# A relational graph layer on one core: one edge tile in 26 fetched row by row instead of one in 28, stores held back, first indices by their own transfer

## The chip, the core and the metric

The kernel runs on one core of a Trainium2 chip. The core has five engines that run side by side and meet at semaphores: TensorE (PE in the profile; PEld is its weight load), VectorE (DVE), ScalarE (ACT), GpSimd (POOL) and SyncE (SP). DMA transfers are issued from the queues of SP, ACT and POOL. The metric is the device time of one execution in microseconds (us); less is better. A time is given as the median of several runs.

## What is computed

The layer takes 12,500 nodes with 256 features, 212,500 edges sorted by destination, and one of 8 relations for each edge. `h` is the normalized and rectified input. An edge brings the row of its source, multiplied by the weight of its relation, to its destination; the node's own row goes through a ninth weight.

```
h = jnp.maximum(_layernorm(x, axis=-1), 0.0)
hx = jnp.einsum('ni,rio->rno', h, weight)
msg = hx[edge_type, src]
agg = jax.ops.segment_sum(msg, dst, num_segments=num_nodes)
out = x + agg * 0.5 ** 0.5 + h_bias + (h @ loop_weight) * 0.5 ** 0.5
```

## The kernel before

**Edges.** The order of sum and product is turned round: source rows are summed for each (destination, relation) first, and the sums are multiplied by the weights once for each group of nodes. The edges stand in 789 units of two tiles with 128 edges each, 1578 tiles in all (the first 80 units are cut plainly, the others overlap a little, so that each covers a narrow range of destinations). For each tile the 128 source rows of 1 KB are brought into one slot of `msg`. There are 66 slots, in pairs of tiles that rotate. VectorE makes one-hot matrices for four tiles at once (`onehots`, L998). TensorE multiplies a tile's rows by its one-hot matrix, four times 128x128 (`edge_sums`, L1036), which sorts them into columns by destination and relation, and VectorE adds a unit's result to the ring of sums `acc` (`add_sums`, L1069).

**Two ways of fetching rows.** Nearly all tiles come by `gather` (L941): one indirect DMA of POOL, which reads 128 row numbers from a column of `gidx` and writes the tile's slot. Every 28th tile (`SINGLE = 28`, tile 27, 55, ...) is left out by POOL. `begin_fetch` books it `FAR = 36` tiles ahead: SP and ACT take 64 of its rows each, load the row numbers into registers, 32 at a time (`load_sources`, L962), and issue a DMA for each row (L970), four items for each queue and tile of the loop (`FETCH`), from `HOLD = 8` tiles after the booking. This begins at tile 152, when the normalized table `h32` is complete for it, and stops 16 tiles before the end. The first 88 tiles are gathered from `x` and normalized in place by ACT (L874); the others are gathered from `h32`.

**How far POOL may run ahead.** `goal(t)` lets the gathers be 64 tiles ahead of the loop at first, fewer later, at least 24, and near the end 8. Each gather also waits for the sums of the unit that stands last in the program before it ("no faster than the sums").

**Groups.** When a group of 128 nodes has its last edge (98 groups, some 16 tiles apart), its products are queued between the edge tiles: two with the loop weight `wl`, then sixteen with `w` (`product`, L1243), into one of two PSUM tiles `po`. Three tiles after the last product `finish` adds bias and result to the rows of x (L1231, L1258) and stores them: four groups at once (L1263), or one by one for the last six and the short first one (L1260). These stores are issued on SP, where the row fetches stand too, and where a store waits until VectorE has added the result. For the last group the products with `wl` stand behind all products of the group before it. At the beginning everything waits for the indices: three transfers on SP (L391), then a cast (L468), a transpose on TensorE and a cast (L432) that make `gidx`, and then POOL's first gather.

**The order of the work** is written by hand in one loop over tiles: a tile's fetches, its sums, then what `issue` takes from the queue of products by a budget, then the late steps such as `finish`.

Of the kernel before, what the change touches and what calls it, by code (L numbers as in the profile page):

```python
# [12 lines left out]
I32 = mybir.dt.int32  # L13
# [7 lines left out]
SP = mybir.EngineType.SP  # L21
# [39 lines left out]
NEXT = 24  # L61
CLOSE = 8

SINGLE = 28
FETCH = 4
SOURCES = 32
BY_SP = (0, 2)
HOLD = 8
FAR = 36
COUNTERS = 4  # L70
LANDINGS = 68

# [177 lines left out]
def kernel(  # L250
# [78 lines left out]
    with ExitStack() as main:  # L329
# [28 lines left out]
        outs = [ps_o.tile([P, 2, D], F32, name=f"po{i}") for i in range(2)]  # L358
        msg, oh, offsets, kind = {}, {}, {}, {}
        firsts, stops, loops, marked, typed, gidx, col = {}, {}, {}, {}, {}, {}, {}  # L360
        added, zeroed, listed = {}, {}, set()
        single, fetches = {}, {SP: [], ACT: []}
        counters = [tc.alloc_semaphore(f"rows{i}") for i in range(COUNTERS)]
        fetched, summed = {}, {}
        landings = [tc.alloc_semaphore(f"landed{i}") for i in range(LANDINGS)]
# [561 lines left out]
        def gather(t):  # L927
            if t % PAIR == 0 and t not in msg:
                room(t)
            if t % QUAD:  # L930
                kind[t] = kind[t - 1]
            else:
                kind[t] = "h" if state["h32"] is not None and t >= state["h32"] + LATE else "x"
            table = {"h": h32, "x": x}[kind[t]]
            b, i, u = place_of(t)
            if single_rows(t) and t not in fetched and t - done["tile"] >= FAR:
                begin_fetch(t)
            if t in fetched:
                return
            at = i * P + u  # L940
            i = nc.gpsimd.indirect_dma_start(  # L941
                out=msg[t], out_offset=None, in_=table[:, :],
                in_offset=bass.IndirectOffsetOnAxis(ap=gidx[b][:, at : at + 1], axis=0))
            if kind[t] == "h":
                n = landed[t] = len(landed)
                i.then_inc(landings[n % LANDINGS], 16)
                tc.no_tile_sem_insts.add(i.ins.name)
                tc.add_to_no_dep_group(f"landed{t}", i.ins)
            if "unit" in latest:
                tc.add_manual_dep(  # L950
                    i.ins, latest["unit"], SYNC_DEP, reason="no faster than the sums")
# [261 lines left out]
        def wrap(g):  # L1213
# [3 lines left out]
            tc.add_manual_dep(i.ins, added[plan.last[g]].name, SYNC_DEP, reason="sums complete")  # L1217
            nc.vector.memset(acc[:, :, :, RING : RING + WIN], 0.0)

        def group_work(g):  # L1220

            d0 = plan.starts[g]
# [10 lines left out]
            def product(r, c, g=g):  # L1233
                n = plan.ends[g] - plan.starts[g]
                if (r, c) == (R, 0):
                    got["out", g] = outs[g % 2][:, 0, :]
                if r == R:
                    while ("self", g) not in got:
# [12 lines left out]
                    tc.add_manual_dep(i.ins, added[plan.last[g]].name, SYNC_DEP, reason="sums complete")  # L1251

            def finish():
                q, k = divmod(g, XG)
                rows_ = got["x", q]
                if g != final:
                    biased(g)
                nc.vector.tensor_add(rows_[:n, k, :], rows_[:n, k, :], got["out", g][:n])  # L1258
                if XG * (q + 2) >= plan.NG or n < P:
                    nc.sync.dma_start(out[d0 : d0 + n], rows_[:n, k, :])  # L1260
                elif k == XG - 1:
                    first = plan.starts[XG * q + shorts(q)]
                    nc.sync.dma_start(  # L1263
                        out[first : d0 + n].rearrange("(k p) d -> p k d", p=P), rows_[:, shorts(q) :, :])
                b = g + SLOTS
                q, k = divmod(b, XG)
                if b < plan.NG:
                    if q < plan.typed:
                        clear(b)
                    else:  # L1270
                        begin(b)
                if q + 1 >= plan.typed and XG * (q + 1) < plan.NG:
                    if k == max(XG // 4, SLOTS - XG * q):
                        load_groups("h", h32, q + 1)
                    if k == XG - 2:
                        mark(q + 1)
                    if k == XG - 1:
                        find_types(q + 1)
# [7 lines left out]
                    work.append((0.55, lambda r=r, c=c: product(r, c)))  # L1286
            work.append((0.0, last))
            if final is not None and g == final - 1:
                work.append((0.0, lambda: biased(final)))
                for c in range(KC):  # L1290
                    work.append((0.55, lambda c=c: product(R, c, final)))
            return work

        with tc.manual_schedule():

            load = prepare(0)
            load[0]()
            for i in range(STAGED):
                load_rows(i)
# [10 lines left out]
            nc.vector.memset(ones_b, 1.0)  # L1310
            nc.vector.memset(zero, 0.0)
            head = len(sources(0, {}))
            for f in load[1 : 1 + head]:
                f()
            for t in range(min(STARTED, NT)):
                gather(t)
            gathered = min(STARTED, NT)

# [127 lines left out]
            for t in range(NT):  # L1446
# [3 lines left out]
                while gathered < min(NT, goal(t)):  # L1450
                    gather(gathered)
                    gathered += 1
                fetch(FETCH)
                blocks_ahead(t)
                credit = min(0.0, credit) + SHARE - (0.52 if t % PAIR else 0.0)
# [78 lines left out]
                step()  # L1534
            while held():
                advance(None)
            state["general"] = nc.values_load(flag[0:1, 0:1], min_val=0, max_val=1)
            while queue or late:
                if late:
                    late.pop(0)[1]()  # L1540
                else:
                    queue.pop(0)[3]()


    with tc.If(state["general"]):
# [26 lines left out]
```

## Time and profile before

| | us |
|---|---|
| median of 3 runs | 1940.45 |
| lowest and highest | 1939.35, 1941.13 |
| the profiled execution, own time | 1939.95 |
| its span, first to last instruction | 1938.2 |

The span is 1.75 us less than the profiled execution's own time, which holds what lies around the program too. In the rows of the profile a line number such as L941 is a line of the kernel; `msg<-h,gidx` names what is written and read; in brackets stands the idle time of the engine before the instruction, and what ended it. "issue" stands for time in which the engine waited for nothing that the profile shows. The mean granted clock of TensorE was 0.955 of full speed. The lines that matter are shown with the prediction.

### The profile page before, as it was taken

The numbers are of one execution on the slowest core, as the hardware profiler recorded it, in microseconds if no ns is written. First come the engines' busy times: TensorE is split into PE (matmuls) and PEld (weight loads), VectorE is DVE, ScalarE is ACT, GpSimd is POOL, SyncE is SP. The second block draws the span as 40 slices with busy tenths as digits, with TensorE's granted clock in tenths as the row PEclk, the third lists the DMA queues.
The fourth block names the chain that finished last, engine by engine and source line by source line (L and its number), as shares of the span: only waits on it lengthen the run. The fifth ranks groups of instructions, "written<-read, shape, count | busy, mean of one in ns | idle before, by whom it ended". The sixth has DMA issues, their size and how long they took to land.

```text
span 1938.2 us, 40494 instructions
## 1 busy us (share of the span) xinstructions
PE 1693.9 (87%) x10152; PEld 1455.2 (75%) x10152; DVE 1315.0 (68%) x3304; ACT 136.4 (7%) x290; POOL 1453.3 (75%) x1554
## 2 busy tenths in 40 slices
PE   2368999999898899889899989898898989899998
PEld 1357889899887787777777778677777778777887
DVE  7879668976667865657766557775566786565543
ACT  6974000000000000000000000000000000000000
POOL 7777777777777777777777777777777777777775
PEclk9568999999999999999999999999999999999999
DMA  9964444444454444453444444444444444444432
GB/s 319 385 216 138 138 132 131 142 134 143 121 154 131 121 142 131 122 150 111 141 132 121 141 132 130 134 118 142 131 120 136 128 135 132 123 141 127 132 118 87
DMA packets 158466, 279.13 MB, mean 144 GB/s; under 512 B 35487, under 2 KB 109330, under 8 KB 158226
## 3 DMA queue, kind: packets, MB, share of 16 engines
q0 software_dynamic: 73344, 200.38, 35.5%
q1 hardware_dynamic: 76744, 72.84, 12.0%
q10 hardware_dynamic: 8138, 3.30, 0.9%
q8 instruction: 80, 1.31, 0.3%
q14 instruction: 160, 1.31, 0.2%
HBM read 250.78 MB, written 25.60 MB: 143 GB/s over the span
## 4 chain that ended last, share of the span: by engine, by line
PE 37%; DMA 22%; POOL 19%; DVE 9%; issue 9%; ACT 3%; SPq 1%; DVEq 0%; POOLq 0%; ACTq 0%; PEldq 0%
DMA msg<-h,gidx 20%; POOL msg L941 19%; PE po L1243 19%; PE ps L1036 17%; DVE acc L1069 2%; ACT msg L874 1%; DVE oh L998 1%; DVE stats L830 1%; SPq L970 1%; DVE acc L1111 1%; ACT xt L874 1%; DVE moves L456 1%; DMA w<-in_L_gnn_weight_dram 1%; DMA xt<-in_x_dram 1%; PE pt L1093 1%
## 5 line engine op out<-in xcount | busy, mean ns | idle before, releaser
L941 POOL DMA_INDIRECT msg<-h,gidx x1440 | 1367.7, 950 | 439.9 <-issue 374.9
L1036 PEld LDWEIGHTS ps<-oh,msg 128*128 128x128 f32 x6312 | 924.9, 197 | 380.0 <-DMA msg<-h,gidx 247.0
L1036 PE MATMUL ps<-oh,msg 128*128 128x136 f32 (+1 forms) x6312 | 1001.9, 289 | 198.8 <-DMA msg<-h,gidx 122.9
L1243 PE MATMUL po<-w,acc 128*128 128x256 f32 (+1 forms) x3136 | 888.7, 389 | 8.7 <-DVE acc L1069 8.3
L1069 DVE TENSOR_TENSOR acc<-acc,ps 128x352 f32 x789 | 408.2, 517 | 387.5 <-PE ps L1036 376.6
L1243 PEld LDWEIGHTS po<-w,acc 128*128 128x128 f32 (+1 forms) x3136 | 519.1, 193 | 47.5 <-issue 11.9
L1111 DVE SCALAR_TENSOR_TENSOR acc<-types,pt 128x256 f32<-128x256 bf16 x720 | 259.6, 414 | 65.5 <-PE pt L1093 55.5
L998 DVE TENSOR_TENSOR oh<-fixed,cols 128x544 f32<-128x544 f32 x395 | 282.7, 716 | 0.0
L1243 PE MATMUL po<-wl,self_t 128*128 128x256 f32 (+1 forms) x392 | 113.5, 415 | 7.9 <-DVE self_t L1098 3.0
L941 POOL DMA_INDIRECT msg<-in_x_dram,gidx x88 | 83.7, 951 | 28.6 <-issue 23.4
L1243 PEld LDWEIGHTS po<-wl,self_t 128*128 128x128 f32 (+1 forms) x392 | 72.4, 206 | 17.2 <-DVE self_t L1098 4.4
L1231 DVE TENSOR_TENSOR xr<-xr,po 128x256 f32<-128x256 f32 (+1 forms) x98 | 40.6, 414 | 16.1 <-PE po L1243 16.1
L1165 DVE CAST types<-pt 128x512 bf16<-128x512 f32 x23 | 15.9, 690 | 50.8 <-PE pt L1161 50.8
L1258 DVE TENSOR_TENSOR xr<-xr,po 128x256 f32<-128x256 f32 (+1 forms) x98 | 41.2, 421 | 10.6 <-PE po L1243 7.3
L874 ACT ACTIVATE msg<-msg,shift,rstd 128x256 f32<-128x256 f32 x88 | 44.8, 587 | 5.0 <-DVE stats L838 3.4
L456 DVE TENSOR_SCALAR moves<-fixed 128x271 int32<-128x271 int32 (+1 forms) x90 | 40.7, 452 | 3.8 <-DVE acc L1069 2.4
L1093 PE MATMUL pt<-ident,hr 128*128 128x128 f32 (+1 forms) x196 | 38.5, 279 | 5.4 <-DVE self_t L1098 2.4
L1098 DVE COPY self_t<-pt 128x256 f32<-128x256 f32 (+1 forms) x98 | 40.8, 416 | 2.8 <-PE ps L1036 1.8
L458 DVE COPY_PREDICATED fixed<-moves,fixed 128x311 int32<-128x311 int32 (+14 forms) x90 | 38.0, 422 | 3.1
L874 ACT ACTIVATE xt<-xt,shift,rstd 128x256 f32<-128x256 f32 x66 | 33.7, 587 | 10.4 <-DVE shift L871 10.4
L1093 PEld LDWEIGHTS pt<-ident,hr 128*128 128x128 f32 (+1 forms) x196 | 25.6, 150 | 7.6 <-DVE self_t L1098 2.5
L1149 DVE TENSOR_TENSOR of<-pt,line 22x512 bf16<-22x512 f32 x23 | 15.7, 682 | 20.7 <-PE pt L1142 20.6
(168 smaller groups left out, 368.1 us busy)
## 6 DMA issues: line engine op xcount, KB each, us to landing
msg<-h ACTq DMA_DIRECT2D x3200, 1.0 KB
msg<-h SPq DMA_DIRECT2D x3200, 1.0 KB
msg<-h,gidx POOLq DMA_INDIRECT x1440
hr<-h SPq DMA_DIRECT2D x23, 512.0 KB
xr<-in_x_dram SPq DMA_DIRECT2D x23, 512.0 KB
out_dram<-xr SPq DMA_DIRECT2D x22, 512.0 KB
xt<-in_x_dram SPq DMA_DIRECT2D x16, 512.0 KB
h<-xt SPq DMA_DIRECT2D x16, 512.0 KB
```

The source lines that it names most:

```text
L456: nc.vector.tensor_single_scalar(m, packed[:, :n], 1 << (bit + k), op=ALU.bitwise_and)
L874: nc.scalar.activation(row, row, AF.Relu, bias=shift[:n, j : j + 1], scale=rstd[:n, j : j + 1])
L941: i = nc.gpsimd.indirect_dma_start(out=msg[t], out_offset=None, in_=table[:, :], in_offset=bass.IndirectOffsetOnAxis(ap=gidx[b][:, at : at ...
L998: j = nc.vector.tensor_tensor(o[:, k : k + v, :i, :width], iota_f[:, :width].unsqueeze(1).unsqueeze(1).to_broadcast([P, v, i, width]), of. ...
L1036: j = nc.tensor.matmul(ps[:, c, first : first + width], m[:, c * P : (c + 1) * P], o[:, :width], start=(i == 0 and c == 0), stop=(end and ...
L1069: i = nc.vector.tensor_tensor(a, a, ps, op=ALU.add)
L1093: in_run("turns", nc.tensor.transpose(pst[:, c, :n], rows_[:n, c * P : (c + 1) * P], ident[:n, :n]), c == KC - 1)
L1098: nc.vector.tensor_copy(got["self", g][:, :, :n], pst[:, :, :n])
L1111: i = nc.vector.scalar_tensor_tensor(acc[:, :, r, s0 : s0 + n], of, float(r + 1), pst[:, :, :n], op0=ALU.is_equal, op1=ALU.mult)
L1231: nc.vector.tensor_add(rows_[:n, k, :], rows_[:n, k, :], outs[g % 2][:n, 1, :])
L1243: i = nc.tensor.matmul(got["out", g][:n], lhs, rhs, start=(r == R and c == 0), stop=(r == R - 1 and c == KC - 1))
L1258: nc.vector.tensor_add(rows_[:n, k, :], rows_[:n, k, :], got["out", g][:n])
```

## The change

One tile in 26 is fetched row by row (`SINGLE`), and booked 40 tiles ahead (`FAR`). The stores of four groups are put on SP's queue 44 tiles of the loop after their sums (`STORE`). The first unit's row numbers come by a transfer of their own on ACT's queue into `direct`, and the first two gathers read them there and are issued before the other indices are turned. The last group's two products with `wl` go to the front of the work of the group before it (with a loop that first issues the `finish` of the group that used the same PSUM tile), and the two stores of the groups before the last are held until all edges are summed.

```
-SINGLE = 28
+SINGLE = 26
-FAR = 36
+FAR = 40
+STORE = 44
...
+            of = direct[:, i : i + 1] if t < PAIR else gidx[b][:, at : at + 1]
             i = nc.gpsimd.indirect_dma_start(
                 out=msg[t], out_offset=None, in_=table[:, :],
-                in_offset=bass.IndirectOffsetOnAxis(ap=gidx[b][:, at : at + 1], axis=0))
+                in_offset=bass.IndirectOffsetOnAxis(ap=of, axis=0))
...
+        def behind(i):
+
+            tc.add_manual_dep(i.ins, latest["unit"], SYNC_DEP, reason="behind the last edges")
...
                 if (r, c) == (R, 0):
+                    while g == final and final - 2 not in finished:
+                        late.pop(0)[1]()
                     got["out", g] = outs[g % 2][:, 0, :]
...
             def finish():
+                finished.add(g)
...
-                if XG * (q + 2) >= plan.NG or n < P:
+                if final is not None and g in (final - 2, final - 1):
+                    alone = rows_[:n, k, :]
+                    stores.append((NT, lambda: behind(nc.sync.dma_start(out[d0 : d0 + n], alone))))
+                elif XG * (q + 2) >= plan.NG or n < P:
                     nc.sync.dma_start(out[d0 : d0 + n], rows_[:n, k, :])
                 elif k == XG - 1:
                     first = plan.starts[XG * q + shorts(q)]
-                    nc.sync.dma_start(
-                        out[first : d0 + n].rearrange("(k p) d -> p k d", p=P), rows_[:, shorts(q) :, :])
+                    to, of = out[first : d0 + n].rearrange("(k p) d -> p k d", p=P), rows_[:, shorts(q) :, :]
+                    stores.append((done["tile"] + STORE, lambda: nc.sync.dma_start(to, of)))
...
             if final is not None and g == final - 1:
+                work = [(0.55, lambda c=c: product(R, c, final)) for c in range(KC)] + work
                 work.append((0.0, lambda: biased(final)))
-                for c in range(KC):
-                    work.append((0.55, lambda c=c: product(R, c, final)))
...
             load = prepare(0)
+            direct = const.tile([P, PAIR], I32, name="direct")
+            with nc.allow_non_contiguous_dma(reason="one unit's indices, a column a tile"):
+                nc.scalar.dma_start(direct, src[:U].rearrange("(i p) -> p i", p=P))
             load[0]()
...
+            for t in range(PAIR):
+                gather(t)
             for f in load[1 : 1 + head]:
                 f()
-            for t in range(min(STARTED, NT)):
+            for t in range(PAIR, min(STARTED, NT)):
                 gather(t)
...
+                while stores and stores[0][0] <= t:
+                    stores.pop(0)[1]()
                 fetch(FETCH)
```

How this moves instructions is seen in the program's order, engine by engine. POOL from its last set-up to the end of the gathers, before and after (`direct` is the new tile of row numbers, `h_57` the table `h32`):

```order
L1304 IOTA tid 128x1
L1305 IOTA tid 128x6
L1307 MEMSET wraps 128x1 x17
L941 DMA msg<-in_x_dram,gidx 128x256 x88
L941 DMA msg<-h_57,gidx 128x256 x1440
```

```order
L1318 IOTA tid 128x1
L1319 IOTA tid 128x6
L1321 MEMSET wraps 128x1 x17
L943 DMA msg<-in_x_dram,direct 128x256 x2
L943 DMA msg<-in_x_dram,gidx 128x256 x86
L943 DMA msg<-h_57,gidx 128x256 x1435
```

Two gathers no longer depend on `gidx`, and there are 1435 gathers from the table instead of 1440.

TensorE in the last 14 tiles, where the products of the last group but one (`po_134`) stand between the edge tiles (`ps`); `po_135` is the last group. Before:

```order
L1036 MATMUL ps_121<-oh,msg 128x104 x2
L1243 MATMUL po_134<-wl,self_t 128x256 x2
L1243 MATMUL po_134<-w,acc 128x256 x2
L1036 MATMUL ps_122<-oh,msg 128x136 x2
L1243 MATMUL po_134<-w,acc 128x256 x4
L1036 MATMUL ps_122<-oh,msg 128x104 x2
L1243 MATMUL po_134<-w,acc 128x256 x4
L1036 MATMUL ps_119<-oh,msg 128x136 x2
L1243 MATMUL po_134<-w,acc 128x256 x3
L1036 MATMUL ps_119<-oh,msg 128x104 x2
L1243 MATMUL po_134<-w,acc 128x256 x3
L1036 MATMUL ps_120<-oh,msg 128x136 x2
```

After:

```order
L1038 MATMUL ps_121<-oh,msg 128x104 x2
L1251 MATMUL po_135<-wl,self_t 128x256 x2
L1251 MATMUL po_134<-wl,self_t 128x256 x2
L1038 MATMUL ps_122<-oh,msg 128x136 x2
L1251 MATMUL po_134<-w,acc 128x256 x4
L1038 MATMUL ps_122<-oh,msg 128x104 x2
L1251 MATMUL po_134<-w,acc 128x256 x4
L1038 MATMUL ps_119<-oh,msg 128x136 x2
L1251 MATMUL po_134<-w,acc 128x256 x3
L1038 MATMUL ps_119<-oh,msg 128x104 x2
L1251 MATMUL po_134<-w,acc 128x256 x3
L1038 MATMUL ps_120<-oh,msg 128x136 x2
```

The last group's loop products now stand ahead of the other's, and the first product with `w` stands one edge tile later. Before, the loop products of the last group stood behind the last row shown.

SP at the end of the changed program, where the rows of the last fetched tile (1559) stand between stores (L1272 stores a group by itself, L1276 four groups, L1270 a held one):

```order
L1188 DMA xr<-in_x_dram 128x2x256
L964 TENSOR_LOAD single
L972 DMA msg<-h_57 1x1024 x11
L1272 DMA out_dram<-xr 128x256
L972 DMA msg<-h_57 1x1024 x21
L964 TENSOR_LOAD single
L972 DMA msg<-h_57 1x1024 x30
L1276 DMA out_dram<-xr 128x4x256
L972 DMA msg<-h_57 1x1024 x2
L1272 DMA out_dram<-xr 128x256
L1270 DMA out_dram<-xr 128x256 x2
```

Of that tile's 64 rows on SP, 53 stand behind the store of group 93, and the two held stores stand behind all rows. Before, the last fetched tile was 1539, and four stores of single groups in a row ended the queue.

More of the change, by code (lines that the diff above doesn't have):

```diff
@@ L360 @@
         firsts, stops, loops, marked, typed, gidx, col = {}, {}, {}, {}, {}, {}, {}
-        added, zeroed, listed = {}, {}, set()
-        single, fetches = {}, {SP: [], ACT: []}
+        added, zeroed, listed, finished = {}, {}, set(), set()
+        single, fetches, stores = {}, {SP: [], ACT: []}, []
         counters = [tc.alloc_semaphore(f"rows{i}") for i in range(COUNTERS)]
@@ L1542 @@
                     queue.pop(0)[3]()
+                while stores:
+                    stores.pop(0)[1]()
     with tc.If(state["general"]):
```

2 lines of the change are left out of this document (added).

## The prediction

> **What bounds the kernel now.** I read the page's shares first, then who waits for whom, then one line's own times, then the stretches.
>
> ```profile
> PE 1693.9 (87%) x10152; PEld 1455.2 (75%) x10152; DVE 1315.0 (68%) x3304; ACT 136.4 (7%) x290; POOL 1453.3 (75%) x1554
> ...
> L941 POOL DMA_INDIRECT msg<-h,gidx x1440 | 1367.7, 950 | 439.9 <-issue 374.9
> ```
>
> By busy share TensorE (PE) looks like the bound, 87% against 75% for GpSimd (POOL). But the 439.9 us of idle before POOL's gathers end in "issue", which is no wait. The list of POOL's waits says it more sharply (engine and line, released by: us in total, times, longest):
>
> ```profile
> POOL msg L941 <- issue: 398.4, 1306, 0.3
> POOL msg L941 <- PE ps L1036: 48.5, 159, 0.3
> ...
> POOL msg L941 <- ACT msg L874: 2.4, 6, 0.9
> ```
>
> The longest gap is 0.3 us whoever is named, with one exception of 0.9. So POOL hands out one gather after the other, 0.95 us each and 0.30 us between. The view of line 941 gives the pace:
>
> ```profile
> L941 POOL DMA_INDIRECT msg<-h,gidx x1440: 942/946/1279, 115.2 to 1921.5; - x180
> ```
>
> From the first start of these 1,440 gathers to the last: (1921.5 - 115.2) / 1439 = **1.2553 us a gather**, the few that take up to 1279 ns included. With 88 gathers from x ahead of them this train runs from 4.7 us to 1922.5 us and has no hole worth a name. The stretches (us; busy time and count of PE, PEld, DVE, ACT, POOL; granted clock, DMA share, GB/s) show where PE stands:
>
> ```profile
> 4.72:166.00 161.28, 73.92 (x335) 64.21 (x336) 133.84 (x473) 122.40 (x260) 121.73 (x128) 0.70 0.89 296
> 166.00:550.00 384.00, 368.99 (x2385) 337.97 (x2383) 287.71 (x703) 12.67 (x30) 290.69 (x306) 0.98 0.47 134
> 550.00:1900.00 1350.00, 1218.52 (x7255) 1024.53 (x7254) 881.69 (x2099) 0.00 (x0) 1021.93 (x1076) 0.98 0.45 131
> ```
>
> Until 166 us PE is held up by the normalizing and the weights and falls behind the gathers; to 550 us it works without a break (369 of 384 us) to catch up; from there it has 10% to spare (1218.5 of 1350 us) and follows the gathers. So a gather less is worth its 1.2553 us, as long as PE's spare time lasts, and what speeds PE up alone is worth nothing before the last few us.
>
> **The change, part by part.**
>
> *One tile in 26.* Tiles 25 + 26k replace 27 + 28k. The first allowed tile is 152 (4-tile rows from 92 - 4 + 64), the last is 1561, so k runs from 5 to 59: 55 tiles instead of 50. The order has 2 + 86 + 1435 = 1523 gathers against 1528. Five fewer: 5 x 1.2553 = **6.28 us off POOL's train**. Their 640 rows go to SP and ACT. What those pay:
>
> ```profile
> L970 SPq DMA_DIRECT2D msg<-h x3200: 227/228/1044, 209.7 to 1871.4; - x189
> ```
>
> A fetched tile costs each queue 64 issues of this line, and two loads of row numbers ahead of them. A slow stretch of SP, quoted with the rivals below, took 13.85 us for 35 rows with such a load among them, 0.396 us a row; at that pace 64 rows take 25.3 us, and 26 tiles last 25 x 1.2553 = 31.4 us. The rows fit, so I take nothing for them. Without that cover PE would wait for the tile's last rows, but POOL is allowed 24 tiles of lead there and would not feel it before PE is some 20 us late.
>
> *Stores 44 tiles later, fetches begun 40 tiles ahead instead of 36.* SP's own waits, longest in total first:
>
> ```profile
> SPq L1263 <- DVE acc L1069: 185.1, 14, 20.0
> SPq L1263 <- DVE xr L1258: 171.4, 9, 57.1
> SPq L1260 <- DVE xr L1258: 88.1, 5, 30.3
> ```
>
> Before, SP stands at a store until its four groups are summed (185.1 + 171.4 us in 23 waits), with the row fetches queued behind it. After, the sums are 44 tiles old when SP comes by, the store waits for nothing, and rows land earlier. That moves waits of SP, and PE's on fetched tiles; neither is on POOL's path: 0. What could be late next is a load into a buffer that a held store still reads; in the new order such a load stands about 27 tiles (some 33 us) of row issues behind that store, so 0 as well.
>
> *First unit's indices by a transfer of their own.* The start, in order of time (start, duration):
>
> ```profile
> 2.87 0.29 DVE L468 CAST sf<-nat_s 128x256 f32<-128x256 int32 x1 [1.72 <-DMA nat_s<-in_src_dram]
> ...
> 4.01 0.42 DVE L432 CAST gidx<-pt 128x256 int32<-128x256 f32 x1 [0.84 <-PE pt L428]
> ...
> 4.72 1.11 POOL L941 DMA_INDIRECT msg<-in_x_dram,gidx  x1 [2.10 <-DVE bound_o L1325]
> ```
>
> POOL waits 2.10 us for the turned indices, so it is free at 4.72 - 2.10 = 2.62. The kernel's first transfer lands at 2.87; one issued at the same moment on ACT's queue, 256 pieces of 4 bytes, the trace does not show. Bounds: it lands with that one and saves up to those 2.10 us, or it is later than 4.72 and costs. I take a start near 3 us. Two gathers then last to 5.5, past 4.43, where the turned indices are ready for the third. But does a start 1.8 us earlier reach the end? Here is the exception of 0.9 us:
>
> ```profile
> 158.36 1.22 PE L1243 MATMUL po<-w,acc 128*128 128x256 f32 x2 [6.51 <-DVE acc L1069]
> ...
> 164.18 0.95 POOL L941 DMA_INDIRECT msg<-h,gidx  x1 [0.30 <-issue]
> 165.54 0.63 PE L1036 MATMUL ps<-oh,msg 128*128 128x136 f32 x4
> 166.02 0.94 POOL L941 DMA_INDIRECT msg<-h,gidx  x1 [0.89 <-ACT msg L874]
> ```
>
> Counted from the start, the gather at 166.02 is that of tile 128. By the order it may not pass tile 63's sums (64 tiles of lead), and PE runs those until 166.0, having stood 6.51 us behind VectorE's bookkeeping just before. POOL lost 0.89 - 0.30 = 0.59 us there already. PE's date at tile 63 comes from weights, norms and VectorE; the gathers are 60 tiles ahead of it. So an earlier start is waited away at this place: **0**, with 2.10 us for the range. Without this wait the gain would be the full 1.8.
>
> *Last loop product sooner, two stores held.* The tail:
>
> ```profile
> 1895.55 0.73 PE L1036 MATMUL ps<-oh,msg 128*128 128x136 f32 x4 [0.66 <-DMA msg<-h,gidx]
> ...
> 1906.49 0.95 POOL L941 DMA_INDIRECT msg<-h,gidx  x1 [0.30 <-issue]
> ...
> 1909.44 0.69 PE L1036 MATMUL ps<-oh,msg 128*128 128x104 f32 x4 [0.71 <-DMA msg<-h,gidx]
> ...
> 1911.30 1.13 PE L1243 MATMUL po<-w,acc 128*128 128x256 f32 x4 [0.29 <-DVE acc L1215]
> ...
> 1921.46 4.19 PE L1036 MATMUL ps<-oh,msg 128*128 128x104 f32 x28
> 1921.51 0.95 POOL L941 DMA_INDIRECT msg<-h,gidx  x1 [0.30 <-issue]
> ...
> 1926.27 7.17 PE L1243 MATMUL po<-w,acc 128*128 128x256 f32 x32 [0.61 <-DVE acc L1069]
> ```
>
> PE last waits for a gather at 1909.44 (tile 1565, twelve before the last), and from there works through but for 0.29 and 0.61 us. The moved product, as many matmuls of the same size as those at 1911.30, now stands ahead of them and fills the 0.29. Nothing else changes in length: **0.29 us**. The price beside it: the last fetched tile, 1559, now lies between PE's wait at 1895.55 and the one at 1909.44. Gather 1565 comes 1.26 us sooner against PE's work there, but PE idled only 0.71 us for it: 1.26 - 0.71 = **0.55 us given back**. The last gather is no new bound: 1921.51 + (1909.44 - 1906.49) = 1924.46, and PE reaches that tile 24/28 through the 4.19 us, at 1925.05. The two held stores are issued after the last edges and before the last sum is ready, while PE is in its 7.17 us: 0.
>
> *Sum.* 6.28 + 0 + 0.29 - 0.55 = 6.02 us. The profiled execution took 1939.95 us (span 1938.2), so 1933.93; the median of the runs is 0.5 us above it, and **1934.4 us** is my forecast, 0.31% faster. What a measurement can tell here is about 0.2%, that is 3.9 us.
>
> **The rivals.**
>
> *The early start passes through.* If tile 63 is done sooner than in the profiled execution, the 1.8 us survive: 1932.6. For it: the wait cost only 0.59 us, and a date that norms and weights set need not be the same in every execution (the three runs span 1.8 us). Against: nothing in the change helps the norms.
>
> *PE takes over.* If PE's spare time is gone where the later fetched tiles fall, for instance because TensorE's clock drops there (0.70 up to 166 us, 0.98 later), POOL's gain of three of five tiles is given back: 2 x 1.2553 = 2.5 us left, 1937.9. Against it stand the 10% of idle from 550 us on.
>
> *The transfers, not their issue, set the pace.* Then rows moved to other queues bring nothing: 1940.4. For it speaks 0.89 of DMA share up to 166 us; against, 0.45 later, where all fetched tiles are, and POOL's even step of 0.95 + 0.30 us. The Trainium skill's page DMA: Bandwidth & Descriptors, section "Issuing engines are not separate DMA queues", states that issuing on several engines saves only the sequencer's time, which is usually small beside the transfer; read alone, it speaks for this case, and by it the sum would be 0. The rows say that here this small time, 1.25 us a tile, is what everything waits for.
>
> *Slower: the last fetched tile comes late.* In the new order 53 rows of tile 1559 stand on SP behind the store of group 93, which waits for that group's sum:
>
> ```profile
> 1854.10 13.85 SPq L970 DMA_DIRECT2D msg<-h  x35
> ...
> 1867.87 0.42 DVE L1258 TENSOR_TENSOR xr<-xr,po 128x256 f32<-128x256 f32 x1
> ```
>
> With this sum ready at 1868.3 the rows are out 53 x 0.396 = 21.0 us later, and landed, with 2.95 us, at 1892.3. PE comes to that tile near 1901 (evenly between 1895.55 and 1909.44): cover 9 us. Beyond that each us is a us at the end; against the time before it decides from 15 us late. The longest wait of such a store was 30.3 us; 10 us more than cover and gain, 25 us late, gives 1950. Against: that sum would have to be later than anything in the tail shows.
>
> **How the numbers follow.** My forecast 0.66, the early start 0.13, PE taking over 0.11, transfers 0.04, the late tile 0.06. The lower end is 1940.45 - 6.28 - 0.29 - 2.10 = 1931.8; the upper one is the second rival, 1937.9; that leaves out the last two cases and little more. Faster by over 0.2% means below 1936.6: the forecast nearly whole, the early start, a little of the second rival, 0.77. Within 0.2%: most of that rival, the transfers, 0.16. Slower: 0.07.
>
> **What would show it.** In the changed kernel's profile: 1,435 + 88 gathers at 1.25 us; the first gather at about 3 us, and at tile 128 a wait grown to 2 us or more, the gather still at 166; SP's waits at stores nearly gone; PE's last wait for a gather before tile 1565 or none there, the wait for line 1215's counterpart gone. I am wrong if POOL shows gaps for PE after 166 us, if the gathers' mean step grows, or if PE waits for fetched rows in the last 100 us.

## The result and the profile after

| | before | changed |
|---|---|---|
| median of 15 runs each, us | 1939.98 | 1935.58 |
| lowest and highest | 1939.05, 1941.55 | 1934.37, 1937.89 |
| the profiled execution (its span) | 1939.95 (1938.2) | 1936.13 (1934.4) |

The ratio is 0.9977, 95% interval 0.9969 to 0.9985: the change makes the kernel 4.4 us, or 0.23%, faster. The forecast was 1934.4 us.

The page's shares, the view of the gathers' line and the list of POOL's waits in the changed kernel (us in total, times, longest):

```profile
PE 1685.5 (87%) x10152; PEld 1479.8 (77%) x10152; DVE 1316.3 (68%) x3304; ACT 136.3 (7%) x290; POOL 1449.5 (75%) x1549
```

```profile
L943 POOL DMA_INDIRECT msg<-h,gidx x1435: 942/946/1273, 115.1 to 1916.2; - x180
```

```profile
POOL msg L943 <- issue: 398.5, 1306, 0.3
...
POOL msg L943 <- PE ps L1038: 48.9, 158, 1.0
...
POOL msg L943 <- ACT rstd L867: 1.5, 2, 1.2
```

POOL still hands out one gather after the other. The train's last gather starts at 1916.2 instead of 1921.5. That is 5.3 us, about the five gathers; the profiled time fell by only 3.8 us. So some 1.5 us were lost behind the last gather, 1.1 of them until the end of PE's last product. The train itself has two longer gaps than before, of 1.0 and 1.2 us. Both stand at the beginning, as the timeline shows (start, duration, engine and line, in brackets the idle time before it and what ended it):

```profile
3.67 1.11 POOL L943 DMA_INDIRECT msg<-in_x_dram,direct  x1 [1.05 <-DMA direct<-in_src_dram]
5.08 0.94 POOL L943 DMA_INDIRECT msg<-in_x_dram,direct  x1 [0.30 <-issue]
...
34.61 0.94 POOL L943 DMA_INDIRECT msg<-in_x_dram,gidx  x1 [1.02 <-PE ps L1038]
...
164.25 0.94 POOL L943 DMA_INDIRECT msg<-h,gidx  x1 [1.16 <-ACT rstd L867]
165.50 0.94 POOL L943 DMA_INDIRECT msg<-h,gidx  x1 [0.30 <-issue]
166.75 0.94 POOL L943 DMA_INDIRECT msg<-h,gidx  x1 [0.31 <-ACT msg L875]
```

The first gather starts 1.05 us earlier (3.67 against 4.72). 0.72 us of it (1.02 - 0.30) are waited away at 34.61, where the gather of tile 24 may not pass the first unit's sums, and 0.86 us at 164.25, at tile 126. Counted from the start, the gather of tile 128 stands at 166.75; before it stood at 166.02.

SP no longer stands at the four-group stores (before: 185.1 and 171.4 us at L1263). Its longest waits are now for PE's sums ahead of a row and for single stores near the end:

```profile
SPq L972 <- PE ps L1038: 85.0, 18, 41.9
SPq L1272 <- DVE xr L1267: 75.6, 3, 39.5
```

PE in the tail of the changed kernel:

```profile
1885.24 0.69 PE L1038 MATMUL ps<-oh,msg 128*128 128x104 f32 x4 [0.45 <-DMA msg<-h,gidx]
...
1890.43 3.02 PE L1038 MATMUL ps<-oh,msg 128*128 128x136 f32 x12 [1.88 <-DMA msg<-h,gidx]
1893.24 1.35 PE L1251 MATMUL po<-wl,self_t 128*128 128x256 f32 x4
...
1906.31 1.91 PE L1251 MATMUL po<-wl,self_t 128*128 128x256 f32 x8
...
1922.05 7.17 PE L1251 MATMUL po<-w,acc 128*128 128x256 f32 x32 [0.61 <-DVE acc L1071]
```

PE last waits for a gather at 1890.43, and for 1.88 us, longer than any wait in the tail before. From there it works without a gap but for the 0.61 us at 1922.05. The wait for L1215's counterpart is gone: the two loop products of the last group now run with the others at 1906.31. Three tiles (x12) at 1890.43 take 3.02 us, though, and the loop products at 1893.24 take 1.35 us where four of the same took 1.03 before:

```profile
1896.12 1.03 PE L1243 MATMUL po<-wl,self_t 128*128 128x256 f32 x4
```

The windows say why (us; busy time and count of PE, PEld, DVE, ACT, POOL; granted clock, DMA share, GB/s), before and changed:

```profile
1885.00:1891.00 6.00, 6.00 (x42) 5.61 (x41) 2.23 (x5) 0.00 (x0) 4.55 (x5) 1.00 0.37 104
1891.00:1897.00 6.00, 4.95 (x38) 4.47 (x37) 3.89 (x8) 0.00 (x0) 4.48 (x6) 1.00 0.41 123
```

```profile
1885.00:1891.00 6.00, 2.69 (x14) 2.15 (x15) 2.35 (x5) 0.00 (x0) 4.71 (x5) 0.96 0.70 219
1890.00:1892.00 2.00, 1.57 (x7) 1.58 (x8) 0.00 (x0) 0.00 (x0) 1.70 (x2) 0.62 0.48 145
1892.00:1894.00 2.00, 2.00 (x10) 1.88 (x10) 0.52 (x1) 0.00 (x0) 1.39 (x3) 0.53 0.33 105
```

In the changed kernel PE is busy only 2.69 of 6 us ahead of 1891, the DMA share is 0.70, and then TensorE's granted clock is 0.62 and 0.53, just behind its last wait, where every microsecond is one at the end.

### The profile page after: what moved, and what is told of

Same layout as the page of the kernel before. It is cut to its first block, busy times and chain, and to the rows that moved or that the text cites. A ratio compares the mean times of both kernels' runs of the same rounds, so it can differ in the third digit from the quotient of the medians.

```text
span 1934.4 us, 41840 instructions
## 1 busy us (share of the span) xinstructions
PE 1685.5 (87%) x10152; PEld 1479.8 (77%) x10152; DVE 1316.3 (68%) x3304; ACT 136.3 (7%) x290; POOL 1449.5 (75%) x1549
## 4 chain that ended last, share of the span: by engine, by line
PE 42%; DMA 27%; POOL 14%; DVE 7%; issue 6%; ACT 2%; SPq 0%; DVEq 0%; POOLq 0%; ACTq 0%
DMA msg<-h,gidx 25%; PE po L1251 22%; PE ps L1038 19%; POOL msg L943 14%; DVE acc L1071 1%; ACT msg L875 1%; DVE acc L1113 1%; DVE stats L831 1%; DMA w<-in_L_gnn_weight_dram 1%; DVE oh L1000 1%; PE pt L1095 1%; DMA h<-xt 1%; DMA xt<-in_x_dram 1%; DVE moves L457 0%; ACT xt L875 0%
## 5 line engine op out<-in xcount | busy, mean ns | idle before, releaser
L1038 PEld LDWEIGHTS ps<-oh,msg 128*128 128x128 f32 x6312 | 944.7, 200 | 341.8 <-DMA msg<-h,gidx 208.5
L1251 PE MATMUL po<-w,acc 128*128 128x256 f32 (+1 forms) x3136 | 894.4, 391 | 12.4 <-DVE acc L1071 11.8
L1071 DVE TENSOR_TENSOR acc<-acc,ps 128x352 f32 x789 | 408.6, 518 | 381.4 <-PE ps L1038 369.4
L1251 PE MATMUL po<-wl,self_t 128*128 128x256 f32 (+1 forms) x392 | 117.5, 426 | 10.0 <-DVE self_t L1100 4.2
```

Of the source, the lines that this page charges most:

```text
L1038: j = nc.tensor.matmul(ps[:, c, first : first + width], m[:, c * P : (c + 1) * P], o[:, :width], start=(i == 0 and c == 0), stop=(end and ...
L1071: i = nc.vector.tensor_tensor(a, a, ps, op=ALU.add)
L1251: i = nc.tensor.matmul(got["out", g][:n], lhs, rhs, start=(r == R and c == 0), stop=(r == R - 1 and c == KC - 1))
```

## The experiments

Each was timed against the kernel before on the same chip; the jobs went to different chips. The first four went to one on which the kernel before takes 2432.7 us, not 1940. All other chips agree on 1939.5 to 1940.1.

| kernel | median, us | less than before, us | ratio, 95% interval |
|---|---|---|---|
| changed | 1935.58 | 4.4 | 0.9977 (0.9969 to 0.9985) |
| stores at once | 1934.98 | 4.7 | 0.9976 (0.9967 to 0.9985) |
| no own index transfer | 1934.99 | 5.1 | 0.9976 (0.9967 to 0.9985) |
| tail as before | 1936.52 | 3.6 | 0.9983 (0.9974 to 0.9992) |
| one in 24 | 1967.46 | -27.4 | 1.0139 (1.0123 to 1.0155) |
| one in 24, loads on ACT | 1965.81 | -26.3 | 1.0138 (1.0123 to 1.0154) |
| one in 25 | 1933.11 | 6.4 | 0.9970 (0.9958 to 0.9982) |
| stores 24 tiles later | 1934.56 | 4.9 | 0.9973 (0.9964 to 0.9982) |
| 57 tiles, 26 and 24 apart | 1932.70 | 6.9 | 0.9963 (0.9950 to 0.9977) |
| *the slow chip:* one in 26 alone | 2492.37 | -59.6 | 1.0248 (1.0204 to 1.0291) |
| *the slow chip:* all but one in 26 | 2419.79 | 12.9 | 0.9953 (0.9930 to 0.9976) |
| *the slow chip:* no own index transfer | 2489.46 | -56.7 | 1.0234 (1.0197 to 1.0271) |
| *the slow chip:* tail as before | 2489.89 | -57.2 | 1.0242 (1.0205 to 1.0279) |

**The slow chip: one in 26 alone, and all but that.** The kernel before with the one number, and the changed kernel with the old number:

```
-SINGLE = 28
+SINGLE = 26
```

```
-SINGLE = 26
+SINGLE = 28
```

> The kernel before with one number changed: one tile in 26 fetched by rows instead of one in 28 (fetches still begin 36 tiles ahead, stores at once, indices and tail as before). Theory (POOL's train sets the pace, 1.2553 us a gather, and the last fetched tile gives some back): 5 gathers fewer, 6.28 less 0.55 to 1.3, so 5.0 to 5.7 us under the kernel before, about 1934.6 where that one takes 1940.0. Rival A (the deferred stores are needed, else PE waits for rows that stand behind SP's stores): 2 us or less under it, 1938 or more. Rival B (PE takes over): about 2.5 us under, 1937.5.

> The changed kernel with one tile in 28 again: later stores, first indices by their own transfer, moved product and held stores are all in. Theory (none of these parts is on the path, and the own transfer makes the gather of the tile that waits for the sums 0.7 us later): between 0.3 us under and 0.7 us over the kernel before, 1939.7 to 1940.7 where that one takes 1940.0. Rival (the early start passes through): 1.8 to 2.1 us under, about 1938.

Neither theory foresaw this. These two kernels ran on the slow chip alone. Here one in 26 costs 2.4%, and the rest of the change gains 0.5%. The first row below is the chain of waits of one in 26 alone, by engine; then two rows of its list of waits:

```profile
SPq 46%; issue 32%; PE 10%; DVE 6%; another core or an unknown queue 3%; ACT 1%; PEld 1%; DMA 1%; DVEq 0%; POOL 0%; PEldq 0%; ACTq 0%
```

```profile
PEld ps L1036 <- PEq L1033: 233.0, 33, 13.3
PEld ps L1036 <- issue: 222.6, 247, 6.7
```

SP, which issues the rows, is the largest part of the chain; in the profile before it had 1%. L1033 (L1035 in the changed kernel) is where PE waits for fetched rows: 233 us, against 7.0 us before on the usual chip. The reason is seen in the view of the fetch line, here of the kernel with all but one in 26, and behind it one row of the kernel before on the usual chip, each with the timeline of SP near 1000 us:

```profile
L972 SPq MOVE msg<-h x3200: 2/29/816, 193.2 to 2342.7; - x189
...
L972 SPq DMA_DIRECT2D msg<-h x3200: 2/204/1405, 260.9 to 2342.7; - x189
```

```profile
1004.46 30.50 SPq L972 DMA_DIRECT2D msg<-h  x49
```

```profile
L970 SPq MOVE msg<-h x3200: 29/29/29, 209.7 to 1871.4; - x189
```

```profile
999.54 20.46 SPq L970 DMA_DIRECT2D msg<-h  x53
```

On the slow chip SP takes 30.50 / 49 = 0.62 us a row, on the usual one 20.46 / 53 = 0.39. A register move takes 29 ns throughout on the usual chip and up to 816 on this one. From first row to last, SP needs (2342.7 - 260.9) / (3199 / 64) = 41.6 us a fetched tile, while 27 gathers last 33.9 us. So the rows are the pace on this chip, and five more fetched tiles can only cost. That the rest of the change gains there fits it: SP need no longer wait at stores (argued, not tried apart). PE shows stalls that nothing explains too (222.6 us of "issue"). What makes these engines stall on this chip stays open, and as all its runs belong to one job, so does whether it was the chip or the time of that job.

**No own index transfer.**

```
-            of = direct[:, i : i + 1] if t < PAIR else gidx[b][:, at : at + 1]
+            of = gidx[b][:, at : at + 1]
...
-            direct = const.tile([P, PAIR], I32, name="direct")
-            with nc.allow_non_contiguous_dma(reason="one unit's indices, a column a tile"):
-                nc.scalar.dma_start(direct, src[:U].rearrange("(i p) -> p i", p=P))
...
-            for t in range(PAIR):
-                gather(t)
```

It ran on the slow chip first, where it tells nothing of its question, and then again:

> The changed kernel without the first unit's own index transfer: the first gather waits for the turned indices again. Theory (an earlier start is waited away, and the own transfer costs 0.7 us through the start of the normalizing): 0.4 to 0.8 us faster than the changed kernel, about 1935.0 where that one takes 1935.6. Rival A (the early start is worth something): 1 to 1.8 us slower than the changed kernel, 1936.6 or more. Rival B (neither matters): the same as the changed kernel. In the profile the theory wants the gather of tile 128 at 166.0 again, against 166.75 in the changed kernel.

> The changed kernel without the first unit's own index transfer, once more, for a chip where the kernel before takes about 1940 us and the changed one 4.4 us less. Theory (an earlier start is waited away at the tiles that wait for the sums, and the own transfer makes the normalizing start later): 4.8 to 5.2 us under the kernel before, the gathers after the wait back at their old times (tile 128 at 166.0 against 166.75 in the changed kernel). Rival A (the early start is worth something): 2.6 to 3.4 us under. Rival B (neither matters): 4.4 us under.

5.1 us under the kernel before. The intervals of this and of the changed kernel overlap almost wholly, so rival B fits as well as the theory. Against rival A (2.6 to 3.4 us) stands the median; only the lower end of the interval, 2.9 us, reaches it. The profiles speak against the theory's second half: the gather of tile 128 starts at 165.77 without the transfer, but also at 165.78 with it, in the kernel with the old tail; it starts between 166.02 and 167.13 with it in three others and between 166.23 and 166.44 without it in four. This date differs from execution to execution by more than the first gather's start does.

**Tail as before.** The edits to `product`, `finish` and the order of `work` are undone:

```
-                work = [(0.55, lambda c=c: product(R, c, final)) for c in range(KC)] + work
                 work.append((0.0, lambda: biased(final)))
+                for c in range(KC):
+                    work.append((0.55, lambda c=c: product(R, c, final)))
```

> The changed kernel with the tail as before: the last group's loop products behind those of the group before, and no store held. Theory (the moved product fills a wait of 0.29 us): 0.3 us slower than the changed kernel, 1935.9 where that one takes 1935.6. Rival (held stores or the moved product cost time at the end, where the changed kernel is 0.8 us longer after its last gather than forecast): 0.4 us or more faster, about 1935.1.

> The changed kernel with the tail as before (last group's loop products behind those of the group before, no store held), once more. Theory (the moved product fills a wait of 0.29 us, held stores nothing; the 0.8 us missing at the end are a stretch of half clock of TensorE behind its last wait, which the tail edits do not touch): 4.1 us under the kernel before, where the changed one is 4.4 under. Rival (the moved product or the held stores cost the missing time): 5 us or more under.

3.6 us under the kernel before, where the changed kernel is 4.4 under: by the medians the tail edits are worth 0.8 us. The intervals (1.6 to 5.0 us here, 2.9 to 6.0 there) overlap, so this tells 0.8 neither from 0.3 nor from nothing. The rival's 5 us or more lie at the far end of the interval and are unlikely.

**Stores at once, and stores 24 tiles later.** The first is the changed kernel with one number; the second also leaves out the own index transfer:

```
-STORE = 44
+STORE = 0
```

```
-STORE = 44
+STORE = 24
```

> The changed kernel, but the stores of four groups are put on SP's queue right behind their sums again (0 tiles later instead of 44). On a chip where the kernel before takes about 1940 us: theory (SP's waits are off the path): the same as the changed kernel within 0.5 us, 4 to 5 us under the kernel before. Rival (rows behind the waiting stores land late, and PE waits for them): 1 to 3 us slower than the changed kernel, 1 to 3 us under the kernel before. On the chip of the first four runs, where the kernel before takes about 2430 us and SP and ACT need 0.6 us a row: SP is the path there, so each wait at a store counts; slower than the changed kernel's 2490 by up to 10 us, the wait at a store in SP's list again.

> The changed kernel without the own index transfer and with the four-group stores 24 tiles later instead of 44, so that the last of them (512 KB) leaves SP ahead of the last fetched tile's rows and not among the last gathers. Theory (that store makes a gather land late, PE idles 1.3 to 1.9 us for it near 1886 and comes out at half clock): no such wait there, 0.5 to 1.5 us faster than without the earlier store, 5.6 to 6.6 us under the kernel before. Rival (TensorE's clock falls behind its last waits anyway): 4.7 to 5.2 us under, half clock for 3 to 4 us between 1886 and 1896 as in the other profiles.

With stores at once the time is that of the changed kernel. SP waits at stores again (128.3 us at L1276 for L1071), and it does not matter. The second was to tell what lengthens the tail. In the changed kernel the last four-group store leaves SP at 1886.08, ahead of the last two rows:

```profile
1886.08 0.41 SPq L1276 DMA_DIRECT2D out_dram<-xr  x1
1886.59 0.65 SPq L972 DMA_DIRECT2D msg<-h  x2
```

With the store 24 tiles later it leaves at 1856.87, and PE's tail reads:

```profile
1890.89 0.73 PE L1038 MATMUL ps<-oh,msg 128*128 128x136 f32 x4 [0.75 <-DMA msg<-h,gidx]
1892.14 2.35 PE L1038 MATMUL ps<-oh,msg 128*128 128x104 f32 x8 [0.52 <-DMA msg<-h,gidx]
```

```profile
1888.00:1891.00 3.00, 1.54 (x9) 1.17 (x10) 1.15 (x3) 0.00 (x0) 2.39 (x3) 1.00 0.51 140
1891.00:1894.00 3.00, 2.38 (x11) 1.92 (x12) 0.85 (x2) 0.00 (x0) 2.25 (x3) 0.73 0.40 124
1894.00:1897.00 3.00, 3.00 (x14) 2.60 (x13) 0.00 (x0) 0.00 (x0) 2.22 (x3) 0.70 0.30 87
```

The wait of 1.88 us is gone, the longest is 0.75. The store did make one gather late: in the three profiles in which it leaves among these gathers (1883.6, 1885.6 and 1886.1) PE waits 1.33, 1.47 and 1.88 us for one some 4 us later, and with stores at once or 24 tiles later never over 0.75 in this stretch. But the clock falls all the same, here to 0.73 and 0.70, and the time is no better than without the earlier store (4.9 against 5.1 us under the kernel before). By the time alone the theory's 5.6 to 6.6 us stand within the interval too (3.5 to 7.0); the profile decides for the rival.

What makes the clock fall can be read from the whole trace of the changed kernel. The clock on record there is 1.0 or 0.5 and changes in steps of 3.41 us. The step ahead of the fall and the step of the fall itself:

```profile
1887.06:1890.47 3.41, 0.96 (x7) 0.59 (x6) 1.16 (x2) 0.00 (x0) 2.50 (x4) 1.00 0.87 282
1890.47:1893.88 3.41, 3.41 (x14) 3.32 (x15) 0.52 (x1) 0.00 (x0) 2.50 (x4) 0.50 0.38 114
```

From 170 us to PE's end there are 27 steps at full clock behind which it fell; PE was busy for at most 0.61 of each of them. Behind 452 others it stayed; PE was busy for at least 0.47 of each of those. The longest pause tells less: one of 1.83 us lies in a step behind which the clock stayed, while in one behind which it fell no pause is over 0.73 us. So it goes by PE's busy share of a step, and between 0.47 and 0.61 either can follow. Nine traces on the usual chips together say the same: 214 falls, all behind a share of at most 0.67, and 4113 steps without one, all at 0.42 or more. The kernel before had such a stretch too, from 1874.4 to 1881.2, but PE caught up with the gathers before it waited again at 1894.20; in the changed kernel the stretch stands behind the last wait.

**One in 24.**

```
-SINGLE = 26
+SINGLE = 24
```

> The changed kernel with one tile in 24 fetched by rows: 59 tiles, four gathers fewer, the last fetched tile is the same 1559. Theory (POOL's train sets the pace): 4 x 1.2553 = 5.0 us faster than the changed kernel, 9.4 us under the kernel before. Rival A (PE takes over, it already ran 10 to 14 us behind the gathers for long stretches of the changed kernel): 2 to 3 us faster than the changed kernel, 6 to 7 us under. Rival B (SP's and ACT's rows no longer fit: 64 rows at 0.396 us are 25.3 us, 23 gathers 28.9 us): slower than the changed kernel, PE waiting for fetched rows.

Rival B, and not by a little: 27 us slower than the kernel before. PE waits for fetched rows 39 times in 59 tiles (in the changed kernel's list there is no such wait), and POOL for PE, up to 5.9 us at once:

```profile
PEld ps L1038 <- PEq L1035: 195.2, 39, 10.8
...
POOL msg L943 <- PE ps L1038: 90.3, 181, 5.9
```

The fetch line and SP's wait there, one in 24 and changed (first and last start):

```profile
L972 SPq DMA_DIRECT2D msg<-h x3776: 227/228/4361, 205.2 to 1919.6; - x199
L972 ACTq DMA_DIRECT2D msg<-h x3776: 227/228/748, 205.2 to 1893.5; - x199
```

```profile
SPq L972 <- PE ps L1038: 58.9, 8, 53.4
```

```profile
L972 SPq DMA_DIRECT2D msg<-h x3520: 227/228/1857, 194.2 to 1887.0; - x196
```

SP waits once for 53.4 us, ahead of its first row, and hardly again. It takes (1919.6 - 205.2) / (3775 / 64) = 29.06 us a fetched tile. Its last row leaves 32.6 us later than in the changed kernel, and the span ends 33.0 us later (1967.4 against 1934.4), and SP has 34% of the chain of waits where it had 1% before: the rows are the path. ACT's queue has one packet of 1 KB in the trace for each row; matched in order, the packets start 2 to 6 us behind their issue in the kernel before (means over 150 us) and about 1 us on the slow chip, where issuing is slower. With one in 24 they start 8 to 10 us behind it from 350 us on, but in the changed kernel it is 3 to 9.5 us, over 8 us in more than half of these stretches. So this lag grows with the rows asked for, and it is not what sets one in 24 apart.

**One in 24, loads on ACT.** It has no own index transfer either.

```
+            queue_ = nc.scalar if q >= 4 else nc.sync
...
-                nc.sync.dma_start(
+                queue_.dma_start(
                     rows_[:, short : len(groups), :],
...
+                    by = nc.scalar if q >= 4 else nc.sync
-                    stores.append((done["tile"] + STORE, lambda: nc.sync.dma_start(to, of)))
+                    stores.append((done["tile"] + STORE, lambda: by.dma_start(to, of)))
```

> One tile in 24 by rows and no own index transfer, but from the 17th group on the loads of the groups' rows and the four-group stores are issued on ACT's queue. Theory (SP's queue set the pace with one in 24: of its 29.1 us a fetched tile 64 rows at 0.369 and two loads of row numbers at 2.31 are 28.2, the rest what is moved here): SP needs 28.2 to 28.6 against 28.9 of the gathers, so PE's waits for fetched rows shrink from 195 us to a few and the time falls from 1967 to between 1930 and 1942. Rival (landing of the rows, PE or the clock limit, not SP's issuing): 1960 or more again.

Nothing was gained: PE waits 199.3 us for rows, in 44 places. The theory's 1930 to 1942 us did not come. SP itself got the room that the theory gave it: its rows come out at the same pace, but it now waits for PE 17.8 (71.2 less the one wait of 53.4 ahead of its first row) and 36.5 us between them, some 0.9 us a tile:

```profile
SPq L972 <- PE ps L1038: 71.2, 19, 53.4
...
SPq L972 <- PEq L1035: 36.5, 12, 9.4
```

Now ACT, which got what SP lost, is as slow as SP was:

```profile
L972 ACTq DMA_DIRECT2D msg<-h x3776: 217/231/2259, 205.9 to 1916.6; - x199
```

That is (1916.6 - 205.9) / (3775 / 64) = 29.0 us a tile, where it was 28.6, and its list shows no wait at the rows. So the queue with these extra transfers in it is the one that is full, whichever it is. Whether issuing or the rows' own way through the queue fills it was not separated.

**One in 25, and 57 tiles.** Both have no own index transfer and stores 24 tiles later. The second takes tiles 26 and 24 apart in turn:

```
-SINGLE = 26
+SINGLE = 25
```

```
-            return (t % SINGLE == SINGLE - 1 and t + 2 * NEAR < NT
+            return (t % 50 in (3, 29) and t + 2 * NEAR < NT
```

> One tile in 25 by rows (tiles 174 to 1549, 56 of them, one gather fewer than the changed kernel), no index transfer of its own, four-group stores 24 tiles later instead of 44; the rest as the changed kernel. Theory (POOL's train as long as SP's queue keeps up: with one in 24 SP took 29.1 us a fetched tile where 23 gathers last 28.9; here 24 gathers last 30.1): 1.3 us for the gather, up to 0.55 because the last fetched tile lies before TensorE's last waits, and what the earlier store brings: 6.5 to 8 us under the kernel before. Rival (SP's queue is the pace here too, or its waits eat the spare 1 us a tile): not faster than the kernel before, PE waiting for fetched rows.

> No own index transfer, four-group stores 24 tiles later, and 57 tiles by rows, in turn 26 and 24 tiles apart (153, 179, 203, 229, ... 1553), so that all of them are the second of their pair of slots and lie before TensorE's last wait for a gather, that of tile 1554. Theory (POOL's train, with SP's and ACT's rows just keeping up at 25 tiles on average): seven gathers fewer than the kernel before ahead of that wait, 7 x 1.2553 = 8.8 us, and 0.3 for the moved product; less up to 1.5 us for a stretch of half clock behind the last waits: 7.5 to 9 us under the kernel before. Rival A (rows come too late where the distance is 24, as with one in 24 throughout): slower than the kernel before, PE waiting for fetched rows in most of the 57 tiles. Rival B (as with one in 25): 6.4 us under.

The kernel with one in 25 does not compute the layer's result (some of its fetched tiles are the first of their pair of slots, which may be the reason), so its time stands only for that amount of work; the 57 tiles put the same distance on the second of the pair alone. At 25 on average the rows just keep up. With the 57 tiles PE waits for them in 12 places, 38.3 us in all, and POOL's lead hides it, since its own longest wait is 1.1 us:

```profile
POOL msg L943 <- PE ps L1038: 47.6, 153, 1.1
PEld ps L1038 <- DVE acc L1071: 42.9, 18, 5.2
PE ps L1038 <- DVE acc L1071: 38.6, 14, 5.0
PEld ps L1038 <- PEq L1035: 38.3, 12, 7.6
```

```profile
1885.00:1891.00 6.00, 5.51 (x40) 4.99 (x39) 3.81 (x8) 0.00 (x0) 4.50 (x5) 1.00 0.43 130
1891.00:1897.00 6.00, 6.00 (x35) 5.46 (x34) 1.68 (x3) 0.00 (x0) 4.72 (x5) 1.00 0.37 109
```

The clock stays at 1.00 in this tail, PE being busy 5.51 of 6 us. From the last gather's start to PE's end it takes 11.8 us here and 11.7 with one in 25, against 12.7 to 14.3 in the five profiles with one in 26 on the usual chips. The 57 tiles bring 6.9 us, between the theory's lower end (7.5) and rival B (6.4). They have the lowest median of all versions; the interval overlaps the changed kernel's.

## Why the prediction was right, and where it was not

**POOL's train.** Right. Five gathers fewer moved the last one forward by 5.3 us. The prediction's 6.28 are there, less about one: the gather of tile 128 stood 0.73 us later in this execution, and the rest lies in the steps behind it. By the profiles of the experiments on the usual chips that date wanders between 165.77 and 167.13, and the start of the last gather, in the four other kernels with one in 26, between 1914.2 and 1918.0. One in 26 alone was not run there. That the gain comes from the train rests on the profile, on the 3.6 to 5.1 us that stay when another part is left out, and on the 6.9 us with two gathers fewer still; the booking 40 tiles ahead was not tried apart.

**The rows that fit.** The 0 came out, its price was wrong. "At that pace 64 rows take 25.3 us, and 26 tiles last 31.4 us" gave a margin of 6 us. The stretch I took it from was 35 rows with one load of row numbers, while a tile has two, and SP has other transfers. With its queue always full SP needs 29.06 us. Then 2.3 us are left at a distance of 26 (31.4), 1.1 at 25 (30.1), and at 24 (28.9) it is 0.2 too long. That the term came out as 0 was luck in so far as my price would have let 24 pass as well. So the change runs with little room; at a distance of 24 the kernel is 27 us slower than before, and on a chip where a row takes 0.62 us the margin is negative. None of my rivals was that the queues of SP and ACT become the pace, though this lies closest to the change, as the ratios of 1.023 to 1.025 on the slow chip show.

**Stores.** Right: SP's waits at stores vanished, and with the stores at once the time is the same. What I did not see is that the last of the delayed stores would go out among the last gathers.

**The early start.** No gain from it is seen, for the reason given: gathers ahead of the sums are waited away. The place was another. I expected the first gather at 3 us and a wait of 2 us or more at tile 128; it was 3.67, and the waits were at tiles 24 and 126.

**The tail.** The mechanism was right, the size off. The 0.29 us wait was filled, PE's last wait stands before tile 1565, and part of the gain was given back because of the late fetched tile. From the last gather's start to PE's end I had 11.93 + 0.55 - 0.29 = 12.2 us; the profiled execution took 13.0. TensorE's clock accounts for the missing 0.8 us and more. Twelve matmuls at 1890.43 took 3.02 us where the same twelve take 2.03 at full clock, with the 57 tiles:

```profile
1887.55 2.03 PE L1038 MATMUL ps<-oh,msg 128*128 128x136 f32 x12 [0.34 <-DMA msg<-h,gidx]
```

The four behind them took 1.35 instead of 1.03, together 1.3 us. The other way, a filled wait brought more than its idle time: the same matmuls take 3.15 us from 1903.16 where they took 4.26 from 1905.71, 0.71 of it idle, and 2.21 from 1906.31 where they took 2.76 from 1909.97, 0.29 of it idle. That is 0.7 us that I did not count. So the step of the tail that failed is "Nothing else changes in length". Without the late fetched tile my terms give 11.93 - 0.29 = 11.6 us; one in 25 and the 57 tiles, at full clock, took 11.7 and 11.8.

**The sum.** 6.02 us were forecast, 4.4 measured, with 2.9 to 6.0 by the interval: its far end is the forecast. In the two profiled executions 3.8 are left: 1.0 is missing in the train and 0.8 in the tail, and 0.4 behind PE's end, where the profiles on the usual chips take between 4.4 and 5.2 us whatever the kernel.

The Trainium skill's rule that the prediction weighed (page DMA: Bandwidth & Descriptors, section "Issuing engines are not separate DMA queues": several issuing engines save only sequencer time) would have given 0. The runs gained by that sequencer time up to 57 tiles, then lost.

## What to carry to other kernels

Before work is moved from a full queue to one that looks idle, measure what the second needs per item when it never rests, from first to last over the whole run, with its other duties in it. The gain is the full queue's price per item until that rate is reached, and turns into a loss of several times the gain one step later. Such a margin can differ from chip to chip, so a version that sits at its edge is worth trying on more than one.

## What the runs showed of the hardware

- One of the five chips of the experiments ran the kernel before 25% slower, in all 17 runs of its one job (2432.7 against 1940 us), with SP's rows at 0.62 instead of 0.39 us. There one in 26 costs 2.4% instead of gaining.
- TensorE's granted clock falls to half without a long pause. In the changed kernel's tail the longest pause ahead of it was 1.88 us; with stores 24 tiles later 0.75 us sufficed. What the falls share is a step of 3.41 us in which PE was busy for 0.61 or less, in the changed kernel's trace. The Trainium skill (page TensorE: Matmul & The Clock Gate, section "Part 1: The HAM clock gate (the "warmup" mystery)") has the halving after at least one idle window of some 3.4 us; the trace differs in that PE was not idle that long ahead of these falls, and it is the busy share of a step that counts.
- Rows of 1 KB on ACT's queue start 2 to 6 us behind their issue with one tile in 28, 3 to 9.5 with one in 26 and, from 350 us on, 8 to 10 with one in 24.
